# Grouping 512-column products and moving single chunks of the down product ahead of third passes

## The chip, the cores and the metric

The kernel runs on one core of one Trainium2 chip. The metric is the device time of one execution in microseconds (us), as the median of several runs. The profile is one further execution, taken by the hardware profiler. Engines are named as in the profile: PE is TensorE (PEld its weight loads), DVE is VectorE, ACT is ScalarE, POOL is GpSimd, SP is SyncE.

## The reference

One transformer-like layer over 4 x 2048 tokens of 256 features, in float32. First a chunked linear attention with a gate, then a feed-forward part whose integer weights are scaled by 1/127, each followed by a residual sum and a layer norm.

```python
Q, K, V = x @ W_q.T, x @ W_k.T, x @ W_v.T            # 8192 tokens, D = 256
S = einsum("bncd,bnkd->bnck", Qc, Kc) * mask         # chunks of 32 tokens, decaying causal mask
O = einsum("bnck,bnkd->bncd", S, Vc)
attn = (sigmoid(x @ W_g.T) * O) @ W_o.T + x
x = layernorm(x + attn)
h = silu(x @ wg.T) * (x @ wu.T)                      # HIDDEN = 768
x = layernorm(x + h @ wd.T)
```

## The kernel before

The 8192 tokens are worked in 16 blocks of 512. The loop at L1173 runs over `b` from 0 to 13 and interleaves three blocks: the feed-forward part of block `b`, the attention of block `n = b + 2` and the first products of block `m = b + 3`. For blocks 1 to 12 (`late` in the code) the order is fully written out by hand: nearly every instruction goes through `in_turn`, which keeps each engine's instructions in the order in which the Python code issues them. There is no planner; the order of the code is the order on each engine.

Precision is kept by splitting operands. A float32 operand of the attention becomes three pieces, `hi`, `lo` and `gap`, and a product becomes three passes that the helper `three` (L535) issues: for each of two PSUM banks the products of kind 0 (`hi`) and kind 1 (`lo`), then a multiplication of that bank in place by ScalarE (L542). The function that it returns issues kind 2 (`gap`) for both banks, the "third pass", which adds to the multiplied banks:

```python
for i, pb in enumerate(banks):
    product(i, pb, 0)
    product(i, pb, 1)
    in_turn(nc.scalar.mul(pb, pb, WHOLE))
```

Four such products occur in a block. `split_gate` (banks `p_g`, gate) and `split_y` (`p_y`) are feature-major: one product streams 512 columns (L501). `split_v` (`p_v`, values) and `split_out` (`p_o`, output of the attention) are token-major: one product streams 256 columns (L523). With `hold=True` the evacuation of the banks is left to a later call (`gate` for `p_g`, `v_copies` for `p_v`).

The feed-forward part has six chunks of hidden features. `ffn_pieces` (L912) gives for each a `high` and a `low` set of 512-column products (L923; four products each, banks `fg` and `fu`), and `silu`, which issues the ScalarE silu (L937) and returns `multiply`: a VectorE product `u` (L948), ScalarE's cast `u_hi` (L953) and GpSimd's `u_lo` (L954). `project_back_late` (L755) is the down product, 256 columns wide (L764, banks `fdn`): `high(chunks)` issues four products for each chunk.

The pieces of the tokens for the next block are `x_hi` on ScalarE (L472), `x_lo` on GpSimd (L476) and `x_gap` on VectorE (L481); `go_hi`, `go_lo` and `go_gap` are the same for the gated attention output `goT`. The function `token_parts` returns `go_gaps`, which issues the two `go_gap` differences.

All accumulators come from one pool of eight PSUM banks; a new tile takes a bank that has been given back, so the order in which tiles are asked for decides who waits for whose evacuation.

In the second half of blocks 1 to 12 TensorE works, before the change, in this order: `low_4`, `low_5`, `high_4`, `p_g` kinds 0 and 1, `p_v` kinds 0 and 1, `p_g` third pass, `high_5`, `p_v` third pass, `p_o` kinds 0 and 1, down chunks 0 and 1, `p_o` third pass, the rest of the down product.

Of the kernel before, what the change touches and what calls it, by code (L numbers as in the profile page):

```python
# [76 lines left out]
def kernel(  # L77
# [18 lines left out]
    KD = D // P  # L96
# [18 lines left out]
    def in_turn(ins):  # L115
        tc.keep_in_program_order(ins)
# [259 lines left out]
    def root_in_turn(mv, kind, name):  # L376
        return root(mv, name, kind[0], order=in_turn)
# [110 lines left out]
    def token_parts(t, name):  # L488
        parts, high, low, difference = pieces_of_tokens(t, name)
        for k in range(KD):  # L490
            high(k)
            low(k)
        return parts, lambda: [difference(k) for k in range(KD)]

    def feature_major(a, b):

# [58 lines left out]
    def split_gate(b, x_parts):  # L555
        sg = work.tile([P, KD, TB], F32, tag="sg", name=f"sg_{b}")

        def finish(i, pb):
            in_turn(nc.scalar.activation(sg[:, i, :], pb, AF.Tanh, scale=HALF))

        return sg, three(f"g_{b}", feature_major(w_parts["wg"], x_parts), finish)
# [226 lines left out]
    def chunked(t):  # L788
        return [t[:, k, :] for k in range(t.shape[1])]
# [290 lines left out]
    sg, gate = attn_gate(0)  # L1080
    gate()
    x_parts, x_gaps = token_parts(xTs[1], "x_1")
# [17 lines left out]
    sg_1, g_rest = split_gate(1, x_parts)  # L1100
# [4 lines left out]
    fd, cast_fd = integers(ffn_dT, ffn_int[2], "fd")  # L1105
# [12 lines left out]
    x_parts, x_gaps = token_parts(xTs[2], "x_2")  # L1118
# [16 lines left out]
    go_parts, go_gaps = token_parts(goT, "go_1")  # L1135
    yT, y_rest = split_y(2, x_parts)
    go_gaps()
    sg, g_rest = split_gate(2, x_parts)
# [4 lines left out]
    gate = g_rest(hold=True)  # L1143
# [6 lines left out]
    x_parts, x_gaps = token_parts(xTs[3], "x_3")  # L1150

    def up_now(b, hT, uT, hc):
        ffn_up(b, hT, uT, range(hc, hc + 1))
# [19 lines left out]
    for b in range(NB - 2):  # L1173
        n = b + 2
        m = b + 3
        more = m < NB
        xns[n] = load_xn(n)
        if b and m + 1 < NB:
            xTs[m + 1] = load_xT(m + 1)
        hT = hTs.pop(b)  # L1180
        uT = ([], []) if b else uT_0
        sT, v, sg = ahead
        if not more:
            scales_next = iterated_scale_and_shift(mv_out, of_out, f"out_{b}")
        late = more and b > 0

        def pieces(hc):
            return ffn_pieces(b, hT, uT, hc)

        if b:  # L1190
            normalize(hs[b + 1], *scales_h)
        if late:
            (high_0, low_0, silu_0), (high_1, low_1, silu_1) = pieces(0), pieces(1)
            low_0()
            low_1()
            high_0()
            silu_0()()
            high_1()
            multiply = silu_1()
        else:  # L1200
            if b:
                up_now(b, hT, uT, 0)
            multiply = ffn_up(b, hT, uT, range(1, 2), held=True)
        if b:
            moving = move_h(b + 1, hs[b + 1])
        else:
            cast_fd(0, range(2, 3))
            multiply()
            x_gaps()
            sT = attn_scores(n, yT)  # L1210
            xTs[m + 1] = load_xT(m + 1)
        if more:
            yT, y_rest = split_y(m, x_parts)
        if b:
            multiply()
        if not more:
            goT = attn_values(n, sT, v, sg)
        multiply = ffn_up(b, hT, uT, range(2, 3), held=True)
        if b > 1:
            normalize(r_before, *scales_out, range(NG // 2))  # L1220
        multiply()
        if more:
            y_rest()
        if b == 0:
            normalize(hs[b + 1], *scales_h)
            moving = move_h(b + 1, hs[b + 1])
        if not more:
            go_parts, go_gaps = token_parts(goT, f"go_{n}")
        multiply = ffn_up(b, hT, uT, range(3, 4), held=True, low_first=not late)
        if b > 1:  # L1230
            normalize(r_before, *scales_out, range(NG // 2, NG))
        multiply()
        if b > 1:
            store(b - 2, r_before)
        if more:
            sT_next = attn_scores(m, yT)
            goT = attn_values(n, sT, v, sg)
            if late:
                (high_4, low_4, silu_4), (high_5, low_5, silu_5) = pieces(4), pieces(5)
                low_4()  # L1240
                low_5()
                go_parts, go_gaps = token_parts(goT, f"go_{n}")
                high_4()
                silu_4()()
                go_gaps()
                sg_next, g_rest = split_gate(m, x_parts)
                v_next, v_rest = split_v(m, x_parts)
                gate = g_rest(hold=True)
                if m + 1 < NB:
                    x_parts, x_high, x_low, x_difference = pieces_of_tokens(  # L1250
                        xTs[m + 1], f"x_{m + 1}"
                    )
                    for k in range(KD):
                        x_high(k)
                high_5()
                multiply = silu_5()
                v_copies = v_rest(hold=True)
                gate()
                multiply()
                if m + 1 < NB:  # L1260
                    for k in range(KD):
                        x_difference(k)
            else:
                multiply = ffn_up(b, hT, uT, range(4, 5), held=True, low_first=True)
                go_parts, go_gaps = token_parts(goT, f"go_{n}")
                cast_fd(1, range(1))
                multiply()
                go_gaps()
                v_next, v_rest = split_v(m, x_parts)
                sg_next, g_rest = split_gate(m, x_parts)  # L1270
                v_rest()
                cast_fd(1, range(1, 2))
                up_with_cast(b, hT, uT, 5, 1, range(2, 3))
        else:
            up_now(b, hT, uT, 4)
            go_gaps()
        r_before = r_out
        if more:
            hs[n], out_rest = split_out(n, go_parts)
            if b:  # L1280
                hTs[b + 1] = split_h(b + 1, moving)
            begun = None
            if late:
                v_copies()
                high, low = project_back_late(b, uT, [chunked(w) for w in fd], "fdn")
                high(range(2))
                begun = high, low, range(2, KH)
            else:
                g_rest()
            mv_h = out_rest()  # L1290
            if b == 0:
                hTs[b + 1] = split_h(b + 1, moving)
            ahead = sT_next, v_next, sg_next
            if m + 1 < NB:
                if late:
                    for k in range(KD):
                        x_low(k)
                else:
                    x_parts, x_gaps = token_parts(xTs[m + 1], f"x_{m + 1}")
            std_h = root_in_turn(mv_h, of_h, f"h_{b}")  # L1300
            if b:
                mv_before, std_before = mv_out, root_in_turn(mv_out, of_out, f"out_{b}")
            back_to_silu()

            def between():
                scales = scale_and_shift(
                    mv_h, std_h, of_h, f"h_{b}", nc.vector, in_turn
                )
                if m + 1 < NB and not late:
                    x_gaps()  # L1310
                return scales

            r_out, mv_out, scales_h = ffn_down(b, uT, hs.pop(b), between, begun=begun)
            if b:
                scales_out = scale_and_shift(mv_before, std_before, of_out, f"out_{b}")
        else:
            multiply = ffn_up(b, hT, uT, range(5, KH), held=True)
            hs[n], out_rest = split_out(n, go_parts)
            multiply()
            hTs[b + 1] = split_h(b + 1, moving)  # L1320
            scales_out = scales_next
            normalize(r_before, *scales_out)
            store(b - 1, r_before)

            def amid():
                return iterated_scale_and_shift(out_rest(), (HALF, 1.0), f"h_{n}")

            r_out, mv_out, scales_h = ffn_down(
                b, uT, hs.pop(b), chunkwise=True, amid=amid
            )  # L1330
            scales_out = iterated_scale_and_shift(mv_out, of_out, f"out_{b + 1}")
# [8 lines left out]
    uT = [], []  # L1340
# [19 lines left out]
    for i in range(2):  # L1360
        groups = range(i * per, (i + 1) * per)
        multiply = ffn_up(last - 1, hTs[last - 1], uT, range(3 + i, 4 + i), held=True)
# [330 lines left out]
```

## Time and profile before

| quantity | value |
|---|---|
| median of 3 runs | 484.53 us (483.99 to 485.03) |
| time of the profiled execution | 485.13 us |
| its span (first to last instruction) | 483.5 us |
| mean granted TensorE clock | 0.997 of full speed |
| TensorE busy | 477.2 us (99% of the span) |
| TensorE weight loads busy | 380.8 us (79%) |
| VectorE, ScalarE, GpSimd busy | 343.2, 370.3, 279.2 us |
| DMA | 36.99 MB, mean 77 GB/s |

The profiled execution has a time of its own, and what is read from its rows is set against that time. The busy time of TensorE is the union of modelled intervals: products are pipelined, so the start of one to the start of the next says more than the length of one. In the timeline a row is the start, the length of a merged group, engine, line, operation, output and inputs, and the count; in square brackets stands the idle time before it and what ended it.

### The profile page before, as it was taken

What the parts mean: (1) busy time and instruction counts of PE and PEld (TensorE: products, weight loads), DVE (VectorE), ACT (ScalarE), POOL (GpSimd) and SP (SyncE); (2) the same over time, 40 slices, a digit from 0 to 9 for tenths busy, and PEclk for the clock granted to TensorE, in tenths of its full rate; (3) what the DMA queues carried; (4) which work ended last, traced back from release to release, by engine and by line L of the source; (5) the groups of instructions that cost most, each with busy time, mean ns of one, the idle gap of its engine ahead of it and who ended that gap; (6) DMA issues with size and microseconds to landing.
All of it is one profiled execution on the core that took longest, in us unless ns stands there. A gap on an engine that the chain in (4) does not pass through costs nothing.

```text
span 483.5 us, 12279 instructions
## 1 busy us (share of the span) xinstructions
PE 477.2 (99%) x4760; PEld 380.8 (79%) x4760; DVE 343.2 (71%) x795; ACT 370.3 (77%) x699; POOL 279.2 (58%) x285
## 2 busy tenths in 40 slices
PE   9999999999999999999999999999999999999995
PEld 5788787787978879697787978878697787968674
DVE  4587958776777766858676777866858676677656
ACT  4878788587877778788786887778788786786845
POOL 2835755655655566455655645565455555557764
PEclk9999999999999999999999999999999999999998
DMA  7730321221313114031321313114031211103102
GB/s 258 234 102 21 107 69 46 55 79 31 109 50 118 45 41 137 26 107 49 102 70 33 109 53 115 45 45 131 23 111 50 83 45 35 56 20 113 37 15 82
DMA packets 43323, 36.99 MB, mean 77 GB/s; under 512 B 4864, under 2 KB 39168, under 8 KB 43264
## 3 DMA queue, kind: packets, MB, share of 16 engines
q1 hardware_dynamic: 42144, 35.28, 23.3%
q10 hardware_dynamic: 1120, 0.92, 0.6%
q8 instruction: 38, 0.62, 0.5%
q14 instruction: 21, 0.17, 0.1%
HBM read 20.45 MB, written 8.39 MB: 60 GB/s over the span
## 4 chain that ended last, share of the span: by engine, by line
PE 98%; DMA 1%; DVE 0%; ACT 0%; issue 0%
PE fg L923 18%; PE fu L923 18%; PE fdn L764 13%; PE p_v L523 9%; PE p_y L501 9%; PE p_o L523 9%; PE p_g L501 9%; PE po L699 4%; PE ps L663 2%; PE fdn L1017 2%; PE fdn L1435 1%; PE fdn L745 1%; PE pg L587 1%; PE pa L811 1%; PE pv L629 1%; PE py L608 1%
## 5 line engine op out<-in xcount | busy, mean ns | idle before, releaser
L954 POOL TENSOR_TENSOR u_lo<-u,u_hi 128x512 f16<-128x512 f32 (+1 forms) x98 | 132.7, 1360 | 94.5 <-ACT u_hi L953 94.4
L948 DVE SCALAR_TENSOR_TENSOR u<-fu,s 128x512 f32<-128x512 f32 (+1 forms) x98 | 66.2, 675 | 76.4 <-ACT s L937 59.0
L953 ACT CAST u_hi<-u 128x512 fp32r<-128x512 f32 (+1 forms) x98 | 59.9, 611 | 36.0 <-DVE u L948 36.0
L937 ACT ACTIVATE s<-fg 128x512 f32<-128x512 f32 (+1 forms) x98 | 57.2, 584 | 15.4 <-PE fg L923 15.4
L923 PE MATMUL fg<-hT_hi,fg_hi 128*128 128x512 f32 (+1 forms) x196 | 67.5, 425 | 0.0
L923 PE MATMUL fu<-hT_hi,fu_hi 128*128 128x512 f32 (+1 forms) x196 | 60.2, 388 | 0.0
L923 PE MATMUL fg<-hT_lo,fg_lo 128*128 128x512 f16 (+1 forms) x196 | 58.0, 377 | 0.0
L923 PE MATMUL fu<-hT_lo,fu_lo 128*128 128x512 f16 (+1 forms) x196 | 57.4, 375 | 0.0
L476 POOL TENSOR_TENSOR go_lo<-goT,go_hi 128x512 fp32r<-128x512 f32 x30 | 39.3, 1331 | 14.4 <-ACT go_hi L472 14.4
L476 POOL TENSOR_TENSOR x_lo<-xT,x_hi 128x512 fp32r<-128x512 f32 x30 | 37.5, 1272 | 15.2 <-ACT x_hi L472 15.2
L481 DVE SCALAR_TENSOR_TENSOR go_gap<-go_hi,goT 128x512 fp32r<-128x512 f32 x30 | 45.0, 1540 | 0.8 <-ACT go_hi L472 0.7
L923 PEld LDWEIGHTS fg<-hT_hi,fg_hi 128*128 128x128 f32 x196 | 36.4, 189 | 9.9
L923 PEld LDWEIGHTS fu<-hT_hi,fu_hi 128*128 128x128 f32 x196 | 36.5, 188 | 8.1
L900 POOL TENSOR_TENSOR hT_lo<-hT,hT_hi 128x512 f16<-128x512 f32 x28 | 35.6, 1294 | 7.7 <-ACT hT_hi L899 7.6
L832 DVE TENSOR_TENSOR h<-p_o,x 128x512 f32<-128x512 f32 x30 | 19.3, 685 | 27.4 <-PE p_o L523 25.2
L923 PEld LDWEIGHTS <-fu_lo 128*128 128x128 f16 x196 | 19.2, 98 | 22.2
L764 PE MATMUL fdn<-fd_hi,u_hi 128*128 128x256 f32 x288 | 36.5, 276 | 0.0
L472 ACT ACTIVATE go_hi<-goT 128x512 fp32r<-128x512 f32 x30 | 17.3, 624 | 22.5 <-DVE goT L718 22.5
L764 PEld LDWEIGHTS fdn<-fd_hi,u_hi 128*128 128x128 f32 x288 | 34.4, 188 | 0.0
L764 PE MATMUL fdn<-fd_lo,u_lo 128*128 128x256 f16 x288 | 33.5, 273 | 0.0
L764 PEld LDWEIGHTS <-u_lo 128*128 128x128 f16 x288 | 27.2, 98 | 3.4
L923 PEld LDWEIGHTS <-fg_lo 128*128 128x128 f16 x196 | 15.0, 98 | 18.3 <-issue 9.4
(179 smaller groups left out, 1066.2 us busy)
## 6 DMA issues: line engine op xcount, KB each, us to landing
x<-in_x_dram SPq DMA_DIRECT2D x16, 512.0 KB, 3.8
xT<-in_xT_dram SPq DMA_DIRECT2D x15, 512.0 KB, 4.2
hT<-sq SPq DMA_DIRECT2D x224, 32.0 KB, 1.9
out_dram<-r SPq DMA_DIRECT2D x13, 512.0 KB, 3.1
out_dram<-r SPq DMA_DIRECT2D x7, 128.0 KB, 1.7
fg_int<-in_ffn_gT_dram SPq DMA_DIRECT2D x3, 256.0 KB, 7.2
fu_int<-in_ffn_uT_dram SPq DMA_DIRECT2D x3, 256.0 KB, 6.4
fd_int<-in_ffn_dT_dram SPq DMA_DIRECT2D x3, 256.0 KB, 5.5
```

Of the source, the lines that this page charges most:

```text
L476: in_turn(nc.gpsimd.tensor_tensor(lo[:, k, :], t[:, k, :], whole, ALU.subtract))
L481: nc.vector.scalar_tensor_tensor(gap[:, k, :], whole, -WHOLE, t[:, k, :], ALU.mult, ALU.add)
L501: nc.tensor.matmul(pb, lhsT=a[kind][:, k, i * P : (i + 1) * P], rhs=b[kind][:, k, :], start=kind + k == 0, stop=True, skip_group_check=True,)
L523: nc.tensor.matmul(pb[:, j * D : (j + 1) * D], lhsT=b[kind][:, k, g * P : (g + 1) * P], rhs=a[kind][:, k, :], start=kind + k + j == 0, sto ...
L699: product = nc.tensor.matmul(po[dims, dc * len(groups) + g, :], lhsT=v[rows, g, dc * P + dims.start : dc * P + dims.stop], rhs=sT[rows, g, :],
L764: nc.tensor.matmul(banks[g // per][:, g % per * D : (g % per + 1) * D], lhsT=part[:, g * P : (g + 1) * P], rhs=w, start=first and g % per ...
L900: nc.gpsimd.tensor_tensor(in_order[1], whole, in_order[0].bitcast(F32), ALU.subtract)
L923: product = nc.tensor.matmul(pb[:, part.start - cols.start : part.stop - cols.start], lhsT=w[kind][:, dc, hc * P : (hc + 1) * P], rhs=hT[k ...
L937: in_turn(nc.scalar.activation(s, pg, AF.Silu, scale=SCALE / H_UP))
L948: nc.vector.scalar_tensor_tensor(u, pu, U_UP / H_UP, s, ALU.mult, ALU.mult)
L953: in_steady_turn(nc.scalar.copy(hi, u))
L954: in_steady_turn(nc.gpsimd.tensor_tensor(lo, u, hi.bitcast(F32), ALU.subtract))
```

## The change

In blocks 1 to 12 the second half is issued in another order. On TensorE: `low_4`, `low_5`, then `p_g` kinds 0 and 1, `high_4`, `p_g` third pass, `high_5`, all 512 columns wide; then, all 256 wide, `p_v` kinds 0 and 1, down chunk 0, `p_v` third pass, `p_o` kinds 0 and 1, down chunk 1, `p_o` third pass, the rest of the down product. The two `go_gap` differences on VectorE are issued apart, one before and one after the `u` of chunk 4. ScalarE has the two `p_g` multiplications ahead of silu 4, silu 5 and the gates ahead of the `p_v` multiplications, and the `x_hi` pair after `u_hi` of chunk 5. The banks of the down product are asked for before those of `p_o`. No instruction is added to or taken from the computation.

```diff
--- before.py
+++ after.py
@@ -490,7 +490,7 @@
         for k in range(KD):
             high(k)
             low(k)
-        return parts, lambda: [difference(k) for k in range(KD)]
+        return parts, lambda ks=range(KD): [difference(k) for k in ks]
 
     def feature_major(a, b):
 
@@ -1240,23 +1240,27 @@
                 low_4()
                 low_5()
                 go_parts, go_gaps = token_parts(goT, f"go_{n}")
+                sg_next, g_rest = split_gate(m, x_parts)
                 high_4()
-                silu_4()()
-                go_gaps()
-                sg_next, g_rest = split_gate(m, x_parts)
+                multiply = silu_4()
+                go_gaps(range(1))
+                gate = g_rest(hold=True)
+                multiply()
+                go_gaps(range(1, KD))
+                high_5()
+                multiply = silu_5()
+                gate()
                 v_next, v_rest = split_v(m, x_parts)
-                gate = g_rest(hold=True)
+                multiply()
+                high, low = project_back_late(b, uT, [chunked(w) for w in fd], "fdn")
+                high(range(1))
+                v_copies = v_rest(hold=True)
                 if m + 1 < NB:
                     x_parts, x_high, x_low, x_difference = pieces_of_tokens(
                         xTs[m + 1], f"x_{m + 1}"
                     )
                     for k in range(KD):
                         x_high(k)
-                high_5()
-                multiply = silu_5()
-                v_copies = v_rest(hold=True)
-                gate()
-                multiply()
                 if m + 1 < NB:
                     for k in range(KD):
                         x_difference(k)
@@ -1281,9 +1285,8 @@
                 hTs[b + 1] = split_h(b + 1, moving)
             begun = None
             if late:
+                high(range(1, 2))
                 v_copies()
-                high, low = project_back_late(b, uT, [chunked(w) for w in fd], "fdn")
-                high(range(2))
                 begun = high, low, range(2, KH)
             else:
                 g_rest()
```

## The prediction

> **What bounds the kernel now.** I read the page first: engine shares, then the chain that ended last.
>
> ```profile
> PE 477.2 (99%) x4760; PEld 380.8 (79%) x4760; DVE 343.2 (71%) x795; ACT 370.3 (77%) x699; POOL 279.2 (58%) x285
> PE 98%; DMA 1%; DVE 0%; ACT 0%; issue 0%
> ```
>
> TensorE is the bound. The change moves only products of blocks 1 to 12, so I measured those: the first low product (`low_0`) of successive blocks starts at 76.74, 105.74, 134.69, 163.65, 192.60, 221.55 us and so on to 424.18, that is 28.95 us a block, to within 0.05 us except the last (28.87). Twelve equal lengths mean no random waiting; what remains is the order itself. Next, the timeline of TensorE in the second half of block 5 (start, length and count; a group's length overlaps the next, so the pitch is the difference of starts):
>
> ```profile
> 208.43 0.62 PE L501 MATMUL p_g<-x_lo,wg_lo 128*128 128x512 f32 x2
> 208.89 0.63 PE L523 MATMUL p_v<-wv_hi,x_hi 128*128 128x256 f32 x4
> 209.36 0.62 PE L523 MATMUL p_v<-wv_lo,x_lo 128*128 128x256 f32 x4
> 209.81 0.62 PE L523 MATMUL p_v<-wv_hi,x_hi 128*128 128x256 f32 x4
> 210.26 0.62 PE L523 MATMUL p_v<-wv_lo,x_lo 128*128 128x256 f32 x4
> 210.72 1.08 PE L501 MATMUL p_g<-x_gap,wg_gap 128*128 128x512 f32 x4
> 211.63 0.62 PE L923 MATMUL fg<-hT_hi,fg_hi 128*128 128x512 f32 x2
> 212.09 0.62 PE L923 MATMUL fu<-hT_hi,fu_hi 128*128 128x512 f32 x2
> 212.56 1.09 PE L523 MATMUL p_v<-wv_gap,x_gap 128*128 128x256 f32 x8
> ```
>
> No hole is left. A 512-column f32 product takes 0.229 us (0.916 for four), a 256-column one 0.1133 (16 of `p_o`, 213.48 to 215.29), so order cannot buy much. What it can buy is in the unmerged starts: at the step from 512 to 256 columns the last wide product takes 0.236 and the next five 0.116, 0.118, 0.119, 0.116, 0.114: 0.023 us too much. `fu` to `p_v` repeats it (0.024). The step back up at 210.72 costs nothing.
>
> What it can lose is the wait ahead of a third pass: ScalarE multiplies a bank in place (L542), and only then may `x_gap` or `go_gap` products add to it. Timelines of ScalarE and of TensorE's weight loads, same block:
>
> ```profile
> 214.64 0.58 ACT L542 ACTIVATE p_o<-p_o 128x512 f32<-128x512 f32 x1
> 215.49 0.58 ACT L542 ACTIVATE p_o<-p_o 128x512 f32<-128x512 f32 x1 [0.27 <-PE p_o L523]
> ```
>
> ```profile
> 215.18 0.98 PEld L764 LDWEIGHTS fdn<-fd_hi,u_hi 128*128 128x128 f32 x8
> 216.09 0.98 PEld L523 LDWEIGHTS p_o<-wo_gap,go_gap 128*128 128x128 f32 x8
> ```
>
> Call S the start of the last `p_o` low product. The next weight load starts with it (215.18). The multiply of the second bank starts at S+0.31 (215.49; 0.04 after the product's end) and ends at S+0.89 (216.07). The ninth load after S starts at S+0.91 (216.09): a load runs one product ahead of its own product. It now belongs to the first bank, long ready.
>
> How soon does a released load start? Block 0 has a true stall of this kind, the multiply of the first `p_v` bank and then the load:
>
> ```profile
> 64.12 0.57 ACT L542 ACTIVATE p_v<-p_v 128x512 f32<-128x512 f32 x1
> 64.74 0.30 PEld L523 LDWEIGHTS p_v<-wv_gap,x_gap 128*128 128x128 f32 x2 [0.41 <-ACT p_v L542]
> ```
>
> The multiply ends at 64.69, the load starts 0.05 later, and TensorE stands: the wait sits on the load, not on the product. Four stalled loads near 40 us show 0.050 or 0.051.
>
> **The change part by part.** *Wide products together.* `p_g` now comes ahead of `high_4`, its third pass ahead of `high_5`, and all 256-column work follows. The same products run, so TensorE's sum stays; one of two steps from 512 to 256 goes: −0.023 us a block. Bounds: 0 (pitches merely redistribute) and −0.04, because the four f32 products after the f16 ones run 0.017 slower at 206 us (`fg`) than at 199.6 (`p_y`), and `p_g` will now stand there. I take −0.023, the row of the very step removed.
>
> *The wait of `p_g`.* The products before it are unchanged up to 206.12. By pitches: `p_g` to 207.95, `high_4` to 208.87, third pass to 209.79, `high_5` to 210.70, `p_v` to 212.54. The multiply of bank 1 starts at 208.15, right after its last product ends, and is done at 208.73; with 0.05 that is 208.78, and its load is due one product early, about 209.10. Free by 0.3 us; cost nothing. Without that cover it would be 0.1 us a block for each 0.1 us.
>
> *ScalarE's and VectorE's new order up to `p_v`.* Steps from this block's rows: silu 4 at 208.67 (after the `p_g` multiplies), VectorE's `u` 0.67 later (209.34), ScalarE's `u_hi` 0.72 later (210.06), silu 5 at 210.59, two gates from 211.06, multiply of `p_v` bank 0 at 212.02, bank 1 possible from 212.54. Data of bank 1 are there at S+0.31 = 212.74. So ScalarE is 0.20 us early and the products set the time. Queued behind the new waits are, on VectorE, one `go_gap` ahead of `u` (1.6 us beside GpSimd, from 206.8 to 208.4, before `u` can start) and one after it (needed only at 216.3); on ScalarE the `x_hi` pair, now 2.4 us later (its takers are `x_gap`, needed next block, and `x_lo` on GpSimd, which still stands behind `hT_lo` until 219.7); `hT_hi` and the `v` copies 0.4 later, with `hT_lo` ready at 219.7 for 221.55. All nothing. No DMA is issued or moved; SP's and GpSimd's orders stay.
>
> *Banks.* In the built order the first down product now takes the banks of silu 4 and `u` 4 (released 209.3 and 210.0, needed 212.5), `p_o` those of silu 5 and `u` 5 (211.2 and 212.3 at worst, needed 213.9 and 214.8). Nothing.
>
> *The wait of `p_v` bank 1.* After S come four down products, four third-pass products of bank 0, then bank 1: its load is due at S+0.91, the place read off above. It is released at S+0.89+0.05, from the ns 0.947 against 0.911: late by 0.036 us. The cover was the `p_g` pass and `high_5`; its load was due over a microsecond after the multiply's end. Bounds: 0.015 (the load started 0.016 after the multiply's end at 216.09, so 0.05−0.035 if the modelled ends are off by a load's jitter) and 0.05.
>
> *The wait of `p_o` bank 1.* The same arithmetic, because only four of eight down products stay ahead of the pass: 0.034 late. But the built order gives this multiply two waits (TensorE, and ScalarE's own gate that used the bank before) where it had one. A second wait goes ahead as a semaphore instruction. The first `p_o` multiply has that form already: in blocks 2 to 12 it starts 0.097 after its product's end, the one-wait multiply 0.036 after. That adds 0.060: late by 0.095. Bounds: 0.03 (no price for the second wait) and 0.12 (0.119 at 20.64 us, the largest two-wait start). I take the eleven identical rows.
>
> *Sum.* 0.036 + 0.095 − 0.023 = 0.108 us a block, 12 blocks: +1.30 us. The profiled execution took 485.13 us (span 483.5, 1.6 around it) and would take 486.4; it lies 0.6 above the median of 484.53, so against the median: 485.8 us, +0.27%. About 0.2%, 0.97 us, is what a measurement of this kernel can tell from no change.
>
> A rule speaks against this. "TensorE: Matmul & The Clock Gate", Part 2, "Step-by-step: what each phase is for", says that TensorE's queue pulls weight loads ahead of products in flight. At 64.74 the load stayed behind the wait, so the row decides; if the load could slip past, both stalls would vanish and the sum would be −0.3 us. The same page, "Back-to-back issue gap", prices a product by its columns alone, with no price for a change of width; by it the saving is 0 and the sum 1.6 us.
>
> **The rivals.** *Not slower: the waits are covered.* If the wait binds the product and not its load, it falls due one pitch later, S+1.02, after both releases (S+0.95, S+1.005), and only 12 × 0.023 = 0.28 us is saved: 484.25. It decides for any due time above S+1.005. For it: f32 loads run 0.11 us ahead in steady flow. Against it: five stalled loads that started 0.05 after the release.
>
> *One stall only.* The second wait's 0.06 is absorbed, since the gate was done long before: (0.036 + 0.034 − 0.023) × 12 = 0.56 us, 485.1, inside the bound. Against it: the first `p_o` multiply waits for an equally old ScalarE result and pays.
>
> *ScalarE falls behind at `p_v`.* Its 0.20 us margin rests on a chain through VectorE. If `go_gap` runs as long as both `go_lo` (to 209.4) and `u` slows beside GpSimd, each 0.1 us beyond the margin adds 1.2 us: 487.0 for the first. For it: `go_gap` means 1.63 us here, `x_gap` 0.64. Against it: 0.9 us between `go_gap`'s end and `u`.
>
> That the change does not do what it says is ruled out by the built order: twelve blocks have the new sequence.
>
> **How the numbers follow.** Forecast 0.68, of which I count 0.06 under the bound because its terms sum from 0.06 us (0.015 + 0.03 − 0.04 a block) to 2.04 us (0.05 + 0.12 − 0); one stall 0.10 (same); covered 0.10 (same 0.08, faster 0.02); ScalarE behind 0.12 (slower). Slower 0.62 + 0.12 = 0.74, same 0.06 + 0.10 + 0.08 = 0.24, faster 0.02. The range runs from 484.9, leaving out the covered case, to 486.9: 2.04 plus 0.3 for the scatter of medians (the runs span 1.0).
>
> **What would show it.** Right: blocks of 29.06 us; the `p_v` load of bank 1 starting 0.05 after its multiply and 0.04 late, that of `p_o` 0.09 late; the second `p_o` multiply 0.10 after its product's end; `p_g` passes without idle. Wrong: blocks of 28.93, or `p_v` multiplies back to back on a ScalarE that is never idle between them.

## The result, and the profile after

The changed kernel takes 488.93 us (median of 4 runs, 488.32 to 489.31) against 484.66 for the kernel before in the same comparison (4 runs, 483.99 to 485.03): +4.27 us, a ratio of 1.0085 with an interval of 1.007 to 1.010. The direction is the predicted one; the size is more than three times the predicted +1.30, and 488.93 lies above the range. The profiled execution took 489.31 us, span 487.8.

The page of the kernel after, engine shares and chain:

```profile
PE 481.3 (99%) x4760; PEld 384.8 (79%) x4760; DVE 334.7 (69%) x795; ACT 374.3 (77%) x699; POOL 276.7 (57%) x285
PE 98%; DMA 1%; DVE 0%; ACT 0%; issue 0%; ACTq 0%
```

TensorE has the same 4760 products and is busy 4.1 us longer; the span grew by 4.3. So almost nothing of the loss shows as idle time: the products themselves come more slowly. Blocks are now 29.22 to 29.30 us long (one 29.61) where they were 28.95.

I summed the times from the start of each product to the start of the next over the twelve blocks, by shape. The 72 narrow f32 products of a block (256 columns) grew from 8.198 to 8.476 us in a typical block, +3.57 in all. The attention's scores and value products grew from 1.787 to 1.867, +0.81 in all. The 48 wide f32 products (512 columns) fell from 11.597 to 11.584, −0.18 in all, and the f16 products stayed. The sum is +4.20, the growth of the span to within 0.1.

The timeline of TensorE in the second half of block 4 shows where the narrow products lose. Its rows answer to those of the prediction (start, length, count; the pitch is the difference of starts):

```profile
181.06 1.08 PE L501 MATMUL p_g<-x_gap,wg_gap 128*128 128x512 f32 x4
181.98 0.62 PE L923 MATMUL fg<-hT_hi,fg_hi 128*128 128x512 f32 x2
182.43 0.62 PE L923 MATMUL fu<-hT_hi,fu_hi 128*128 128x512 f32 x2
182.89 0.63 PE L523 MATMUL p_v<-wv_hi,x_hi 128*128 128x256 f32 x4
183.36 0.63 PE L523 MATMUL p_v<-wv_lo,x_lo 128*128 128x256 f32 x4
...
184.78 0.63 PE L764 MATMUL fdn<-fd_hi,u_hi 128*128 128x256 f32 x4
185.25 1.10 PE L523 MATMUL p_v<-wv_gap,x_gap 128*128 128x256 f32 x8
186.19 0.63 PE L523 MATMUL p_o<-wo_hi,go_hi 128*128 128x256 f32 x4
...
188.07 0.63 PE L764 MATMUL fdn<-fd_hi,u_hi 128*128 128x256 f32 x4
188.54 1.17 PE L523 MATMUL p_o<-wo_gap,go_gap 128*128 128x256 f32 x8
189.54 1.98 PE L764 MATMUL fdn<-fd_hi,u_hi 128*128 128x256 f32 x16
191.37 2.79 PE L764 MATMUL fdn<-fd_lo,u_lo 128*128 128x256 f16 x24
```

The timeline of the kernel before, block 5, for its `p_o`:

```profile
213.48 0.62 PE L523 MATMUL p_o<-wo_hi,go_hi 128*128 128x256 f32 x4
...
215.29 1.07 PE L764 MATMUL fdn<-fd_hi,u_hi 128*128 128x256 f32 x8
```

Sixteen `p_v` products take 184.78 − 182.89 = 1.89 us, 0.118 each; in the kernel before they took 1.83, five slower ones at the step included, and the sixteen of `p_o` 215.29 − 213.48 = 1.81 (0.1133 each). The `p_g` third pass runs without a hole (181.06 to 181.98), as predicted. The loss isn't a passing cost at the step to narrow products either: `p_o`, two microseconds later, also takes 1.88. Only behind the `p_o` third pass do sixteen down products run at 0.114 again. There are two pitches for the same product, 0.1133 and 0.1178, and a stretch keeps the one that it has. Ten of the twelve blocks begin `p_v` in the slow one. Block 5 begins in the fast one:

```profile
212.67 0.62 PE L523 MATMUL p_v<-wv_lo,x_lo 128*128 128x256 f32 x4
213.13 0.62 PE L523 MATMUL p_v<-wv_hi,x_hi 128*128 128x256 f32 x4
213.58 0.62 PE L523 MATMUL p_v<-wv_lo,x_lo 128*128 128x256 f32 x4
214.04 0.62 PE L764 MATMUL fdn<-fd_hi,u_hi 128*128 128x256 f32 x4
214.49 1.12 PE L523 MATMUL p_v<-wv_gap,x_gap 128*128 128x256 f32 x8
215.45 0.63 PE L523 MATMUL p_o<-wo_hi,go_hi 128*128 128x256 f32 x4
215.92 0.63 PE L523 MATMUL p_o<-wo_lo,go_lo 128*128 128x256 f32 x4
```

The starts are 0.45 or 0.46 apart up to `p_v`'s third pass and 0.47 behind it. The pitch turns at the late load in that pass. The granted clock is not the reason; the windows of a slow, a fast and another slow stretch of the kernel after have the same (PEclk). Nor is it DMA, which is busiest in the fast stretch (a share of 1.05 against 0.59 and 0.12):

```profile
core 0: us, PE busy (x) PEld busy (x) DVE busy (x) ACT busy (x) POOL busy (x), PEclk, DMA share, GB/s
182.89:188.54 5.65, 5.65 (x49) 5.65 (x48) 2.59 (x3) 4.91 (x11) 2.60 (x2) 1.00 0.59 193
212.67:214.49 1.82, 1.82 (x18) 1.82 (x17) 0.69 (x1) 1.74 (x5) 0.90 (x1) 1.00 1.05 340
215.45:217.81 2.36, 2.36 (x23) 2.36 (x21) 1.90 (x2) 1.74 (x4) 1.26 (x1) 1.00 0.12 45
```

The late loads themselves are there. The list of the third passes by tile gives minimum, median and maximum length of a product in ns: `p_v` in block 5 (fast before the pass) and `p_o` in block 4 (slow before it), of the kernel after:

```profile
L523 PE MATMUL p_v<-wv_gap,x_gap x8: 276/280/312, 214.5 to 215.3; 128*128 128x256 f32 x8
L523 PE MATMUL p_o<-wo_gap,go_gap x8: 280/281/337, 188.5 to 189.4; 128*128 128x256 f32 x8
```

The same row of the kernel before, block 5:

```profile
L523 PE MATMUL p_o<-wo_gap,go_gap x8: 276/276/276, 216.2 to 217.0; 128*128 128x256 f32 x8
```

One product is held by 0.036 (312 against 276) at `p_v` and by 0.056 (337 against 281) at `p_o`. The median also tells the pitch: 276 in the fast one, 281 in the slow one.

### The profile page after: what moved, and what is told of

It reads as the page before. It is cut to its first block, busy times and chain, and to the rows that moved or that the text cites. A ratio compares the mean times of both kernels' runs of the same rounds, so it can differ in the third digit from the quotient of the medians.

```text
span 487.8 us, 12268 instructions
## 1 busy us (share of the span) xinstructions
PE 481.3 (99%) x4760; PEld 384.8 (79%) x4760; DVE 334.7 (69%) x795; ACT 374.3 (77%) x699; POOL 276.7 (57%) x285
## 4 chain that ended last, share of the span: by engine, by line
PE 98%; DMA 1%; DVE 0%; ACT 0%; issue 0%; ACTq 0%
PE fg L923 18%; PE fu L923 18%; PE fdn L764 13%; PE p_o L523 9%; PE p_v L523 9%; PE p_y L501 9%; PE p_g L501 9%; PE po L699 4%; PE ps L663 2%; PE fdn L1017 2%; PE fdn L1438 1%; PE fdn L745 1%; PE pg L587 1%; DMA wg<-in_w_gT_dram 1%; PE pv L629 1%; PE pa L811 1%
## 5 line engine op out<-in xcount | busy, mean ns | idle before, releaser
L954 POOL TENSOR_TENSOR u_lo<-u,u_hi 128x512 f16<-128x512 f32 (+1 forms) x98 | 124.2, 1273 | 82.2 <-ACT u_hi L953 78.4
L923 PE MATMUL fg<-hT_hi,fg_hi 128*128 128x512 f32 (+1 forms) x196 | 65.1, 413 | 0.0
L476 POOL TENSOR_TENSOR go_lo<-goT,go_hi 128x512 fp32r<-128x512 f32 x30 | 45.3, 1528 | 14.4 <-ACT go_hi L472 14.4
L481 DVE SCALAR_TENSOR_TENSOR x_gap<-x_hi,xT 128x512 fp32r<-128x512 f32 x30 | 28.1, 974 | 26.5 <-ACT x_hi L472 26.5
L764 PE MATMUL fdn<-fd_hi,u_hi 128*128 128x256 f32 x288 | 39.0, 278 | 0.0
L764 PEld LDWEIGHTS fdn<-fd_hi,u_hi 128*128 128x128 f32 x288 | 35.8, 188 | 0.0
L481 DVE SCALAR_TENSOR_TENSOR go_gap<-go_hi,goT 128x512 fp32r<-128x512 f32 x30 | 23.4, 788 | 9.2 <-ACT go_hi L472 9.1
```

The lines of the kernel that those rows point to most:

```text
L476: in_turn(nc.gpsimd.tensor_tensor(lo[:, k, :], t[:, k, :], whole, ALU.subtract))
L481: nc.vector.scalar_tensor_tensor(gap[:, k, :], whole, -WHOLE, t[:, k, :], ALU.mult, ALU.add)
L764: nc.tensor.matmul(banks[g // per][:, g % per * D : (g % per + 1) * D], lhsT=part[:, g * P : (g + 1) * P], rhs=w, start=first and g % per ...
L923: product = nc.tensor.matmul(pb[:, part.start - cols.start : part.stop - cols.start], lhsT=w[kind][:, dc, hc * P : (hc + 1) * P], rhs=hT[k ...
L954: in_steady_turn(nc.gpsimd.tensor_tensor(lo, u, hi.bitcast(F32), ALU.subtract))
```

## What has to be told apart

Three things may have cost the time, and the trace alone mixes them. First, the two late loads, as predicted. Second, the slow pitch: either the single down chunks and stalls cause it, or the longer run of wide products ahead of `p_v` does, without any stall. Third, the scores, for which the order of GpSimd's work came under suspicion. The timelines of VectorE and GpSimd at the end of a block, first VectorE and then GpSimd of the kernel before, then both of the kernel after:

```profile
220.92 0.78 DVE L388 TENSOR_SCALAR minus_h<-rstd_h 128x4 f32<-128x4 f32 x1
...
221.82 0.69 DVE L998 SCALAR_TENSOR_TENSOR r<-fdn,h 128x512 f32<-128x512 f32 x1
```

```profile
219.19 2.49 POOL L476 TENSOR_TENSOR x_lo<-xT,x_hi 128x512 fp32r<-128x512 f32 x2
```

```profile
193.28 1.24 DVE L388 TENSOR_SCALAR minus_h<-rstd_h 128x4 f32<-128x4 f32 x1
...
194.64 0.69 DVE L998 SCALAR_TENSOR_TENSOR r<-fdn,h 128x512 f32<-128x512 f32 x1
```

```profile
192.02 2.48 POOL L476 TENSOR_TENSOR x_lo<-xT,x_hi 128x512 fp32r<-128x512 f32 x2
```

`minus_h` is a 128x4 operation that takes 0.17 us alone. Here it ends about when GpSimd's `x_lo` ends (221.68 and 194.50). Against the start of the next block (221.55 and 194.00), `x_lo` ends 0.13 late before and 0.50 late after; the residual `r` starts 0.27 and 0.64 late. The chain that begins with it leads to the next block's `p_y` and its copies `yT`, which the scores read: VectorE's second `yT` copy ends 0.29 us ahead of the first score product before (231.26 against 231.55), and at 204.09, after the scores have begun, in the kernel after. The 64 score products answer: 0.69 to the first value product before (231.55 to 232.24), 0.77 after. TensorE, the kernel before and below it the kernel after:

```profile
231.55 0.76 PE L663 MATMUL ps<-yT,xT 128*32 128x32 f32 x64
232.24 1.16 PE L699 MATMUL po<-sT,v 64*64 64x64 f32 x64
```

```profile
204.00 0.84 PE L663 MATMUL ps<-yT,xT 128*32 128x32 f32 x64
204.77 1.16 PE L699 MATMUL po<-sT,v 64*64 64x64 f32 x64
```

## The experiments

**Single chunks in the old order.** The kernel before, with only the second part of the change.

```diff
+                high, low = project_back_late(b, uT, [chunked(w) for w in fd], "fdn")
+                high(range(1))
                 v_copies = v_rest(hold=True)
                 gate()
...
+                high(range(1, 2))
                 v_copies()
-                high, low = project_back_late(b, uT, [chunked(w) for w in fd], "fdn")
-                high(range(2))
```

> The order before, with only the second half of the change: one down chunk ahead of the third pass of p_v, one ahead of that of p_o. Twelve 512-column f32 products stand ahead of p_v, as before. Theory A (the place in a cycle of three wide products at which the wide stretch ends sets the pitch of the narrow ones): p_v and p_o keep 0.1133 to 0.1145 us, the p_o load of bank 1 is late by 0.09 us and nothing else changes but the scores, blocks of 29.04 to 29.13, +1.1 to +2.2 us. Theory B (single chunks with their late waits slow the narrow products): p_o at 0.118 as after the change, blocks near 29.3, +4 us.

Measured: 487.47 us against 484.81, ratio 1.0055 (1.0038 to 1.0071); +2.66 lies between the forecasts of the two theories. Eleven of twelve blocks enter `p_v` in the fast pitch, and `p_o` runs at 0.1133. So the single chunk does not make the slow pitch at the entry. It does make the late `p_o` load, here in the fast pitch for which the prediction had costed it; the third pass of block 9 by tile:

```profile
L523 PE MATMUL p_o<-wo_gap,go_gap x8: 276/277/381, 334.0 to 334.9; 128*128 128x256 f32 x8
```

The load starts 0.015 ahead of its product instead of 0.110, so it is 0.095 late, as predicted, and the product is held for 0.100. But the sixteen down products behind it then run at 0.118: another 16 × 0.0045 = 0.07 us. A typical block is 0.22 longer.

**Two chunks ahead of each third pass.** The changed kernel with the covers back: eight down products instead of four.

```diff
-                high(range(1))
+                high(range(2))
...
-                high(range(1, 2))
+                high(range(2, 4))
...
-                begun = high, low, range(2, KH)
+                begun = high, low, range(4, KH)
```

> The change with two down chunks ahead of each of the two third passes (0 and 1, then 2 and 3), so that no load waits for ScalarE. Still 20 wide f32 products ahead of p_v. Theory A: nothing breaks the slow pitch, so all 72 narrow f32 products of a block run at 0.118 instead of 0.1138: +0.30 us a block, and the scores a little later than after the change, +4 to +5 us against before. Theory B: without late waits the narrow products are at 0.1133, blocks of 28.93 to 29.0, within 0.6 us of before.

Measured: 494.31 us, ratio 1.0204 (1.0186 to 1.0222): worse. No load is late any more, and yet nine of twelve blocks run slow from the first `p_v` product to the end of the f32 down products. The other three run fast throughout, in the same execution. The timeline of TensorE, block 5 and below it block 10:

```profile
213.29 0.64 PE L523 MATMUL p_v<-wv_hi,x_hi 128*128 128x256 f32 x4
...
217.06 0.63 PE L523 MATMUL p_o<-wo_hi,go_hi 128*128 128x256 f32 x4
...
219.88 1.11 PE L523 MATMUL p_o<-wo_gap,go_gap 128*128 128x256 f32 x8
```

```profile
362.38 0.63 PE L523 MATMUL p_v<-wv_hi,x_hi 128*128 128x256 f32 x4
...
366.03 0.62 PE L523 MATMUL p_o<-wo_hi,go_hi 128*128 128x256 f32 x4
...
368.75 1.07 PE L523 MATMUL p_o<-wo_gap,go_gap 128*128 128x256 f32 x8
```

From the first `p_v` to the `p_o` third pass the same 56 products take 6.59 and 6.37 us. A block's narrow products take 8.486 in the slow blocks and 8.181 to 8.190 in the fast ones: 0.3 us for the pitch alone. That is the control that the trace of the change could not give: no stall, same code, two pitches. The rest of the loss lies elsewhere: the scores and value products take 2.26 us a block instead of 1.79, and the wide f16 products about 0.1 more. The `p_o` pass, which the chain to the scores starts from, now comes eight products later; that this is the reason is argued, not shown.

**The number of wide products ahead of `p_v`.** If the run of wide products chooses the pitch, its length should matter. Before the change 12 wide f32 products stand unbroken ahead of `p_v`, after it 20. Three kernels repeat the first `p_g` product of the changed kernel once, twice or three times; a fourth repeats it twice in the kernel before.

```diff
         banks = [bank(f"p{i}_{name}") for i in range(2)]
+        for _ in range(again):
+            product(0, banks[0], 0, range(1))
...
```

> The change with the first p_g product of each block issued twice (the second overwrites the first): 21 wide f32 products ahead of p_v. Theory A: the stretch ends at the place at which it ended before the change, so p_v falls to 0.1133 after some five products (mean 0.1145) in all twelve blocks, until the late load of p_v. Theory C (neighbouring engines slow the narrow products): p_v stays at 0.118. Time against after the change: 12 x 0.229 for the products less 12 x 0.07 to 0.1 by A, +1.6 to +1.9 us; +2.7 us by C.

> The same with two repeats: 22 wide f32 products. Theory A: the remaining place of the three; the two odd blocks of the changed kernel (at 212 and 241 us) ended there and were fast, so p_v has a mean of 0.1145 to 0.115. Theory C: 0.118 again.

> The change with the first p_g product issued four times (three repeats): 23 wide f32 products, the same place in the cycle of three as the change's 20. If the count by threes decides the entry, p_v is slow again (0.118) in about ten of twelve blocks, against two of twelve with one repeat and five with two. If only small differences of time decide it, fast and slow blocks are mixed as with two repeats.

> The order before with the first p_g product of each block issued three times (two repeats): 14 wide f32 products ahead of p_v, the same remainder by three as the change's 20. If the count by threes decides the entry, p_v starts slow (0.118) in most of the twelve blocks, where the order before has none, and third pass of p_v, behind a new entry, is unchanged at 0.1155. If the change's neighbouring work decides it, p_v stays at 0.1144.

One run each, in this order: 490.35, 496.09, 498.94 and 491.09 us. These times hold the repeated products (0.229 us each, so 2.7 to 8.2 us in twelve blocks) and what those delay, so only the pitch at the entry is read:

| wide f32 products ahead of `p_v` | kernel | blocks that enter fast, of 12 |
|---|---|---|
| 12 | before | 12 |
| 12 | single chunks in the old order | 11 |
| 12 | before, `x_lo` early (below) | 11 |
| 20 | the change | 2 |
| 20 | two chunks ahead | 3 |
| 20 | the change, `x_lo` early (below) | 3 |
| 21 | the change, one more | 10 |
| 22 | the change, two more | 7 |
| 23 | the change, three more | 3 |
| 4 | two kernels with `low_5` moved (below) | 12 and 12 |
| 14 | before, two more | 1 |

The last row shows it without any other part of the change; the timeline of the kernel before with two repeats, block 9:

```profile
329.06 0.63 PE L523 MATMUL p_v<-wv_hi,x_hi 128*128 128x256 f32 x4
...
330.94 1.10 PE L501 MATMUL p_g<-x_gap,wg_gap 128*128 128x512 f32 x4
...
333.74 0.62 PE L523 MATMUL p_o<-wo_hi,go_hi 128*128 128x256 f32 x4
...
335.55 1.07 PE L766 MATMUL fdn<-fd_hi,u_hi 128*128 128x256 f32 x8
```

`p_v` takes 1.88 for sixteen and is slow; `p_o`, behind another run of wide products, takes 1.81. Counts that leave 0 when divided by three mostly enter fast, those that leave 2 (14, 20, 23) mostly slow. The unmerged starts give a hint why three: successive wide products start 0.226, 0.229 and 0.232 us apart, over and over. At 182.67 us in the kernel after the last wide product takes 0.227 and the next 0.117, and all that follow 0.1178; in the kernel before the last wide one takes 0.236, and after five products the pitch is 0.1133. So the place in this cycle at which the width changes matters. The count alone is not the rule: 4 and 22 both leave 1, and enter fast in 24 of 24 and in 7 of 12 blocks; in the old order eight wide products, which leave 2, stand between `p_v` and the narrow products behind it, and all 48 of these stretches, in four kernels, run on in the fast pitch. The place itself separates them without an exception. Blocks 1 to 12 of the twelve kernels have 192 steps from wide to narrow f32 products; at all 57 that lead into the slow pitch the last wide product takes 0.226 or 0.227, behind one of 0.231 to 0.233, and at all 135 that lead into the fast one it takes 0.230 to 0.236. What in the engine makes the cycle and holds the pitch no profile row shows.

**`x_lo` ahead of `hT_lo` on GpSimd.** The same edit in the kernel before and in the changed one, to test the third suspicion.

```diff
+            if late and m + 1 < NB:
+                for k in range(KD):
+                    x_low(k)
             if b:
                 hTs[b + 1] = split_h(b + 1, moving)
...
-                if late:
-                    for k in range(KD):
-                        x_low(k)
-                else:
+                if not late:
```

> The order before with x_lo on GpSimd ahead of hT_lo. By theory D the score load that waits for yT before the change (TensorE's start of the scores 0.309 us after the last wide product, 0.216 without a wait) no longer waits: up to 0.09 us a block, 1.1 us faster than before, 483.6 to 484.2 against 484.8. If yT is late for another reason: no change.

> The change with x_lo on GpSimd ahead of hT_lo, so that GpSimd is done before VectorE's minus_h. Theory D (minus_h stands until GpSimd's x_lo ends, and so yT and the score products come late): minus_h near 0.2 us in place of 1.24, the score and value products back from 1.865 to 1.79 us a block or less, 0.9 to 2 us faster than after the change. Rival (the scores are late because ScalarE's square root comes late): no change. The narrow products stay at 8.48 us a block by both.

In the changed kernel: 487.72 us against 485.18, ratio 1.0062 (1.0047 to 1.0078). GpSimd ends the last of `x_lo` and `hT_lo` 10.66 us ahead of the first score product of block 5, where it was 9.50 (192.23 to 202.89; 194.50 to 204.00). VectorE at the end of block 4 shows it:

```profile
192.51 0.17 DVE L388 TENSOR_SCALAR minus_h<-rstd_h 128x4 f32<-128x4 f32 x1
...
192.80 0.69 DVE L998 SCALAR_TENSOR_TENSOR r<-fdn,h 128x512 f32<-128x512 f32 x1
```

The operation takes 0.17 us again, and the scores and value products about 1.80 a block instead of 1.867. The narrow products stay at 8.46: this part and the pitch are separate. In the kernel before, the edit gives 485.14 against 485.18, ratio 1.0005 (0.9995 to 1.0014): no change. `minus_h` falls from 0.78 to 0.26 us and the scores stay at 1.787 in a typical block; `yT` had 0.29 us in hand there. The same delay is free on one side of that margin and costs 0.08 us a block on the other.

**All three causes taken away.** The changed order with two chunks ahead of each pass, `x_lo` early, and `low_5` (f16) moved to stand right ahead of `high_5`, so that only four wide f32 products precede `p_v`. The second kernel keeps the single chunks.

```diff
                 low_4()
-                low_5()
...
                 go_gaps(range(1, KD))
+                low_5()
                 high_5()
```

> The change with two down chunks ahead of each of the two third passes, low_5 moved right ahead of high_5 (four wide f32 products between the f16 ones and p_v, and no product more or less), and x_lo ahead of hT_lo. No load waits for ScalarE. If the entry is fast in all blocks, narrow products at 8.19 us a block, 484 to 485.5; if slow in most, 8.49 and 3.5 us more. By theory D the scores stay near 1.79 to 1.9 and not at 2.26 as with two chunks alone.

> The change with low_5 right ahead of high_5 and x_lo ahead of hT_lo, single chunks kept. Against the run with two chunks at each place it has the late waits back. The entry should be fast in all blocks (0.1135), then the p_v load is 0.036 us late and the p_o load 0.06 to 0.10 late; each late load may turn the pitch to 0.118 for the products behind it. From the late loads alone 0.13 us a block; with the pitch turned from p_v's third pass to the end of the f32 products up to 0.13 + 44 x 0.0045 = 0.33. Scores at 1.79 to 1.81.

With all three: 486.60 us against 485.18, ratio 1.0039 (1.0023 to 1.0054), above the 484 to 485.5 expected for a fast entry in all blocks. All twelve blocks enter fast and no load is late: the narrow products take 8.168, which is 0.030 less than in the kernel before. The prediction gave 0.023 to the wide products together. It is not a gain in total: the wide products, f32 and f16 together, take 16.364 instead of 16.338, the scores and value products 1.871 (that the later `p_o` pass is the reason is again argued, not shown), and 0.9 us are lost once, behind the twelve blocks, 0.7 of it where a `p_o` set waits for `go_lo` on GpSimd. Blocks are 29.033. With no late load, here and with two chunks ahead above, each of the 24 blocks keeps the pitch of its entry up to the `p_o` third pass.

With the single chunks kept: 487.57 against 485.17, ratio 1.0054 (1.0037 to 1.0071). All blocks enter fast; then the late `p_v` load stretches its pass to 0.120 a product, and behind it six blocks run slow and six fast. The late `p_o` load follows in every block. Narrow products take 8.43 to 8.50, with one exception of 8.356: the two late loads and the pitch that they turn cost about 0.28 us a block, where the waits alone were predicted at 0.13. No version beat the kernel before.

## Why the prediction was wrong in size

By its own steps, for a typical block, in us:

| step of the prediction | predicted | measured in the change |
|---|---|---|
| wide products together | −0.023 | −0.013 (wide), +0.222 (pitch of the narrow ones) |
| wait of `p_g` | 0 | 0 |
| ScalarE's and VectorE's order | 0 | +0.080 (scores) |
| wait of `p_v` bank 1 | 0.036 | 0 slow, 0.036 fast |
| wait of `p_o` bank 1 | 0.095 | 0.056 slow (0.095 in the fast pitch, single chunks in the old order) |
| sum | 0.108 | 0.345 |

The 0.222 is the growth of the narrow products, 0.278, less the held `p_o` product, 0.056. So of the 0.345 only 0.056 is a wait that the prediction had summed; that the change came out slower owes more to the two failures below than to the predicted terms.

**The step that failed** is "wide products together". It took five slow products at the step from 512 to 256 columns as the whole price of that step, and 0.1133 as the pitch of everything behind. Its bounds, 0 and −0.04, left out that the order could change the pitch of some fifty products. All rows read for it came from stretches that had entered in the fast pitch. The prediction read a price by columns alone in the Trainium skill, "TensorE: Matmul & The Clock Gate", Part 2, "Back-to-back issue gap". The section gives a gap for each number of columns, and says that in a stream of weight loads and products both set the spacing. In this case columns and weight loads were not enough: the same 56 products took 6.59 and 6.37 us in two blocks of the kernel with two chunks ahead.

**The second failure** is "all nothing" for the work that the new order delays. It followed `hT_lo` to its own taker at the next block's start, and stopped there. It missed that VectorE's small operations stretch while GpSimd works (`minus_h` from 0.17 to 1.24 us), so that a later `x_lo` delays the residual, `yT` and the scores: 0.8 us in twelve blocks. For this the cover was 0.29 us, and was not named.

**The late loads** were right. Loads stay behind the wait: the load starts 0.050 after ScalarE's end at `p_v` in every block, and the multiplication with two waits starts 0.097 after its product's end (but for block 6, below). In the kernel after, block 5, the multiplication (first row, ends 214.82) and the load that it releases:

```profile
214.24 0.58 ACT L542 ACTIVATE p_v<-p_v 128x512 f32<-128x512 f32 x1
```

```profile
214.87 0.19 PEld L523 LDWEIGHTS p_v<-wv_gap,x_gap 128*128 128x128 f32 x1
```

In the slow pitch the load is due later, at S + 9 × 0.1178 − 0.115 = S + 0.945 instead of S + 0.910, so the slow pitch hides most of the `p_v` wait and a third of the `p_o` wait. That is why the two measured terms are smaller than predicted although their mechanism held.

**The rivals.** The waits were not covered, and the second wait of the `p_o` multiplication was paid. In eleven of twelve blocks ScalarE was not behind at `p_v`: the multiplication of bank 1 starts 0.037 after its product's end in block 4, and ScalarE has been idle for 0.12 us ahead of it, of the 0.20 that the prediction had worked out. In block 11 it was: silu 4 starts 0.28 us later than in block 10, the chain through VectorE carries that to the first `p_v` multiplication, and the second starts 0.100 after its product's end. The `p_v` third pass takes 0.06 longer there, but the pitch is the fast one behind it, and the block is no longer than its neighbours (29.29). None of the rivals was the cause.

**One thing stays open.** Block 6 took 0.3 us more. The chain of waits there, in order of time:

```profile
246.80 0.02 ACTq L542
246.82 0.32 issue
247.14 0.59 ACT p_o L542
```

ScalarE has its semaphore instruction behind it at 246.82 and starts the multiplication 0.32 later, for no reason that the profile shows; in the other blocks it is 0.04. The late silu 4 of block 11 (386.45) is a second such hold, 0.32 behind its semaphore instruction. The kernel before has one, at 342 us, which costs it 0.034. Why they fall there isn't settled.

## What to carry to other kernels

Where TensorE is 99% busy and no wait is seen, compare the pitch of identical products from stretch to stretch before pricing a new order: 4% on some fifty products a block weighed more here than both new waits together. A weight load that waits should be released more than one product ahead of its use (loads led by 0.11 us here), and a stall costs more than itself when it turns the pitch of what follows. When a change delays work on a side engine, follow the delay past its own taker, through the engines that work beside it, to the first place where the margin is used up.

## What the runs showed of the hardware that was not expected

- Narrow f32 products (128x256) had two lasting pitches at a granted clock of 1.00, 0.1133 and 0.1178 us; weight loads then led their products by 0.110 and 0.115. A run of wide products, or a stalled load, could change it: with 12 and 21 wide ones ahead 44 of 48 blocks entered fast, with 14, 20 and 23 only 12 of 60. Wide f32 products started 0.226, 0.229 and 0.232 us apart in turn, and all 57 slow stretches of 192 began behind a last wide product of 0.226 or 0.227.
- A 128x4 operation of VectorE took 0.17 us alone and 0.78 or 1.24 beside a 128x512 operation of GpSimd, and ended as that one did.
- ScalarE started an instruction 0.32 us after its semaphore instruction, 0.28 later than in other blocks, with nothing in the profile that it waited for: twice in the profiled execution of the change (blocks 6 and 11), and at the same `p_o` multiplication of block 6 in six of the experiments' kernels.
